# Gate and up projections by Strassen's seven block products in a hybrid attention kernel

## The chip, the core and the metric

The kernel runs on one core of one Trainium2 chip. The core has a tensor engine (PE, with its weight loads shown apart as PEld), a vector engine (DVE), a scalar engine (ACT), GpSimd (POOL), and a sync engine (SP) that issues the DMAs. Each engine works through its own queue in order and waits on semaphores for the others. The metric is the device time of one execution in microseconds. Before the change it is 2567.37 us, the median of three runs (2565.67 to 2568.33).

## The reference

Sixteen sequences of 512 tokens by 256 channels, all float32, go through four stages, each with a layer norm in front and a residual sum behind: a windowed attention (called a below), a feed-forward (f), a rotary attention (b), and the same feed-forward with the same weights again (h). The change is to the feed-forward:

```python
def _L0_ffn_ref(x, w_gate, w_up, w_down):
    DIM = 256
    HIDDEN = 768
    SCALE = 1.0 / 127.0
    wg = _dequant(w_gate, x.dtype)
    wu = _dequant(w_up, x.dtype)
    wd = _dequant(w_down, x.dtype)
    gate = jnp.einsum('bsd,hd->bsh', x, wg)
    up = jnp.einsum('bsd,hd->bsh', x, wu)
    h = jax.nn.silu(gate) * up
    return jnp.einsum('bsh,dh->bsd', h, wd)
...
x = x + _L0_attn_a_ref(_layernorm(x, axis=-1), ...)
x = x + _L0_ffn_ref(_layernorm(x, axis=-1), ...)
x = x + _L0_attn_b_ref(_layernorm(x, axis=-1), ...)
x = x + _L0_ffn_ref(_layernorm(x, axis=-1), ...)
```

## The kernel before, in words

**Order of the work.** The Python code does not emit its instructions in the order in which it is written. Every piece of work is a generator that yields an `Op` (an engine, a duration that the author assumes, what it needs, which buffers it takes and gives back). `Plan.run` keeps a clock per engine, always takes the operation that can start first on it (among those within a small window, by rank and then by `progress`, which the tables `LEAD`, `ENDS` and `SHARE` shift stage by stage), and only then lets the generator emit its instructions. So the queue order of every engine is fixed at build time by the planner's assumed durations, and on the chip each queue is followed strictly. All sixteen sequences are in flight as a pipeline over the four stages: while one sequence is in stage b, the next are in a and f and the one before is in h.

**PE fillers.** If the planner finds PE without work for over `FILL = 1.2` us, `Plan.run` calls `fill`, which emits `int((gap - 0.35) / 0.22)` matmuls of the identity with itself, 128 columns wide, whose result nobody reads.

**Ways in which PE is used.** A product of 128 by 128 weights with a moving operand can lie as one instruction on the whole array (FULL), or as four instructions on four strips of 32 output columns, which run side by side (COLS). Attention scores (`dn`, `nm`, `sa`) lie on four strips of 32 rows (ROWS). `product` (L485) emits the first two; an `Op` with `lying=FLEX` takes FULL or COLS, whichever suits what PE did last.

**PSUM.** It has eight banks of 512 float32 per partition. An operation that takes `"u"` gets one of them (six at most may be held so), one that takes `"s"` gets four, for the four strips of a score block. Dependences between the engines are tracked by tile, and a tile here is a whole bank.

**Feed-forward of one sequence** (`feed_forward`). `normalize` (L503) makes `xn` on DVE (L529), transposes it on PE into two banks (L563), and DVE (L571) and ACT (L573) copy one bank each into `xnt`, channels on the partitions, 512 tokens along the free dimension. Then for each of the six blocks of 128 hidden channels, `channels` emits two products of 512 columns (two blocks of input channels, summed in PSUM) for gate, and two for up. ACT takes tanh of half the gate (L1099), DVE multiplies (tanh + 1) by the gate (L1101), and DVE multiplies that by up into `ht` (L1107). When all six are done, four `project_out` calls, six products of 256 columns each, give the output, which DVE adds to the residual (L601). The last sequence's stage h goes in two halves of 256 tokens (`parts_of`), so that its end is shorter.

**Buffers.** Apart from constants, tiles live in slots that the planner hands out: `in_a`, `in_b`, `in_f` for `xnt` of the stages, `xn`, three `tmp`, four `pt` for transposed attention weights, two `ptb`, and so on.

Of the kernel before, what the change touches and what calls it, by code (L numbers as in the profile page):

```python
# [15 lines left out]
P = 128  # L16
S = 512
# [66 lines left out]
EARLY = {"us": 110.0}  # L84
BORDER = {"fr": 0.30, "fc": 0.15, "rf": 0.21, "rc": 0.13, "cf": 0.21, "cr": 0.21}
NEVER = 1e9

class Plan:
# [17 lines left out]
    def ready(self, op):  # L106
        at = 0.0
        for n in op.needs:
            at = max(at, self.at.get(n, NEVER) if isinstance(n, str) else n)
        for tag in op.takes:  # L110
            n = {"uu": 2, "s": 4}.get(tag, 1)
            if tag in ("u", "uu", "s"):
                at = max(at, sorted(self.slots["bank"])[n - 1])
            if tag != "s":
                at = max(at, sorted(self.slots["u" if tag == "uu" else tag])[n - 1])
        return at
# [7 lines left out]
    def take(self, op):  # L124

        for tag in op.takes:
            if tag == "s":
                op.k[tag] = [self.pick("bank") for _ in range(4)]
            elif tag in ("u", "uu"):
                op.k["u"] = [(self.pick("u"), self.pick("bank")) for _ in tag]  # L130
                op.k["u"] = op.k["u"] if tag == "uu" else op.k["u"][0]
            else:
# [9 lines left out]
    def progress(self, thread):  # L142

        _, _, stage, seq, _ = thread
        return seq + LEAD[stage] + ENDS.get(f"{stage}{seq}", 0.0) + self.done.get((stage, seq), 0.0) / SHARE[stage]

# [6 lines left out]
    def turn(self, op):  # L153
# [4 lines left out]
        return TURN[self.lying[0] + lying[0]]  # L158

    def run(self):  # L160
        while True:
# [17 lines left out]
            if first:  # L179
# [13 lines left out]
                <= least + (TURN["hold"] if engine == "pe" and self.lying == ROWS == c[1][1].lying else 0.05)  # L193
            ]
            if engine == "pe":
                start, t = min(
# [55 lines left out]
TURN = {"hold": 0.25, "fr": 0, "fc": 0.15, "rf": 0.2, "cf": 0.2, "rc": 0.05, "cr": 0.05}  # L252
LEAD = {"a": 0.0, "f": 0.741, "b": 1.33, "h": 2.645}

ENDS = {"b0": -0.05, "b2": -0.29, "h0": -0.04, "a0": 0.57, "a1": -0.08, "f15": -0.26, "h13": -0.11}
# [3 lines left out]
def kernel(  # L259
# [101 lines left out]
    def load_raw(ap, n, tag, name):  # L361
        raw = work.tile([P, n, ap.shape[1]], I32, tag=tag, name=f"raw_{name}")
        nc.sync.dma_start(raw, ap.rearrange("(c p) e -> p c e", p=P))
        return raw, const.tile([P, n, ap.shape[1]], F32, tag=name, name=name)

    raw_wg, wg_sb = load_raw(w_gate, NC, "ptb0", "wg_sb")
    raw_wu, wu_sb = load_raw(w_up, NC, "ptb1", "wu_sb")
    raw_wd, wd_sb = load_raw(w_down, NF, "ht0", "wd_sb")
# [49 lines left out]
    def dequantized():  # L418

        for at, t, raw, by, name in (  # L420
            (19.0, wg_sb, raw_wg, DEQUANT, "wg"),
            (22.0, wu_sb, raw_wu, DEQUANT, "wu"),
            (25.0, wd_sb, raw_wd, 0.5 * DEQUANT, "wd"),
        ):
            op = yield dve(0, at, us=0.9, makes=name, sbuf=True)
            if name == "wd":
                plan.slots["ht"] = [op.end]
            nc.vector.tensor_scalar(t, raw, by, None, ALU.mult)
# [4 lines left out]
    def values_bias():  # L433
# [3 lines left out]
        for kc in range(NC):  # L437
# [15 lines left out]
            "xn": 1,  # L453
            "in_a": 1,
            "in_b": 1,
            "in_f": 1,
            "tmp": 3,
            "pt": 4,
# [24 lines left out]
    input_of = {"a": "in_a", "b": "in_b", "f": "in_f", "h": "in_f"}  # L483
# [18 lines left out]

    def normalize(stage, b):  # L503
# [3 lines left out]
        slot = input_of[stage]  # L507
        for n, tokens in enumerate(parts_of(stage, b)):
# [3 lines left out]
            for t in tiles:  # L512
                op = yield dve(0, needs[t], us=0.51)
                if t == 0:
                    xt = xs[b]
                    stats = work.tile([P, NT, 6], F32, tag=f"stats_{stage}", name=f"stats_{me}")
                    mv = work.tile([P, NT, 2], F32, tag=f"mv_{stage}", name=f"mv_{me}")
                    rstd = work.tile([P, NT], F32, tag=f"rstd_{stage}", name=f"rstd_{me}")
                nc.vector.bn_stats(stats[:, t, :], xt[:, t, :])
                nc.vector.bn_aggr(mv[:, t, :], stats[:, t, :])  # L520
# [3 lines left out]
            takes = ("xn",) if n else ("xn", slot)  # L524
            op = yield dve(0, op.end, us=0.375 * len(tiles), takes=takes, sbuf=True)
            k_xn = op.k["xn"]
            xn = work.tile([P, NT, D], F32, tag="xn", name=f"xn_{me}_{n}")
            for t in tiles:
                nc.vector.tensor_scalar(  # L529
                    xn[:, t, :],  # L530
# [21 lines left out]
            else:  # L552
                plan.at[f"bias_{me}"] = 0.0
            for c in range(NC):
# [4 lines left out]
                    gives=(("xn", k_xn),) if c == NC - 1 else (),  # L559
                )  # L560
                ps = bank(op, [P, S], f"lt_{me}_{n}_{c}")
                for t in tiles:
                    nc.tensor.transpose(  # L563
                        ps[:, t * P : (t + 1) * P], xn[:, t, c * P : (c + 1) * P], ident
                    )
                if c == n == 0:
                    xnt[me] = work.tile([P, NC, S], F32, tag=slot, name=f"xnt_{me}")

                def keep(_, c=c, ps=ps, tokens=tokens):
# [5 lines left out]
                how = dict(gives=(("u", op.k["u"]),), makes=f"xnt_{me}.{n}.{c}")  # L575
                plan.start(
                    one((dve if c == 0 else act)(width, op.end, **how), keep), stage, b, -1
                )
# [3 lines left out]
        "f": ["wg", "wu", "wd"],  # L582
# [84 lines left out]
    def window_attention(b):  # L667
# [45 lines left out]
        yield from values("a", b, v_all, wv_sb, 0, v_lock, (("in_a", 0),))  # L713
# [181 lines left out]
    def weighted(b):  # L895
# [15 lines left out]
        def turns():  # L911
            for t in range(NT):
                for n, (oc, par) in enumerate(parts):
                    op = yield pe(0.44, f"sc_{me}.{t}.0", f"sc_{me}.{t}.1", takes=("u", "pt"))
# [9 lines left out]
                    def keep(_, t=t, n=n, on_dve=on_dve, ps=ps, op=op):  # L924
                        pt = buf(op, "pt", [P, 4, P], f"pt_{b}_{t}_{n}")
# [4 lines left out]
                        pts[t, n] = pt, op.k["pt"]  # L930
# [26 lines left out]
        for t in range(NT):  # L957
            go(weights(t))
            for ns in (range(4),):
# [10 lines left out]
                op.gives = [("pt", pts[t, n][1]) for n in ns]  # L970
# [45 lines left out]
    def global_queries(b, qg, keys, v_all, v_lock):  # L1016
# [30 lines left out]
        for c in range(NT):  # L1047
            nc.tensor.transpose(tp[:, c, :], gp[:, c * P : (c + 1) * P], ident[:R, :R])
        op = yield act(NT * R, op.end, takes=("pt",), gives=(("u", op.k["u"]),))
        pg = buf(op, "pt", [P, NT, R], f"pgq_{b}")  # L1050
# [8 lines left out]
            gives=(("pt", op.k["pt"]), (v_lock, 0)),  # L1059
# [27 lines left out]
    def feed_forward(stage, b):  # L1087
# [5 lines left out]
        def gated(f, n, tokens, gate, k, at):  # L1093

            width = tokens.stop - tokens.start
            op = yield act(width, at, takes=("tmp",))
# [472 lines left out]
```

## Time and profile before

| What | Value |
|---|---|
| median of the runs | 2567.37 us |
| the profiled execution, time | 2566.21 us |
| its span, first to last instruction | 2564.2 us |
| mean granted PE clock | 0.997 of full |
| PE busy | 99% of the span |
| DVE busy | 60% |
| ACT busy | 58% |
| POOL busy | 37% |
| gate and up products: 2916 records in stage f, 2388 in h | 184.6 + 184.4 and 183.7 + 184.2 us busy |
| DMA | 50.88 MB, mean 20 GB/s |

Busy time is the union of an engine's instructions. A float32 product shows as two records on PE for each instruction of the program (a transpose as one), and some of the records can be missing. Ends of matmuls are modelled, so the distance from one start to the next says more than the length of a record. Idle time is told apart by what ended it. A window names microseconds from the first instruction.

### The profile page before, as it was taken

The page shows a single profiled execution, that of the slowest core. Times are in us where ns is not written, and L with a number is a line of the kernel's source. Part 1 is how long each engine was busy: PE and PEld are TensorE (multiplying, and loading weights), DVE is VectorE, ACT ScalarE, POOL GpSimd, SP SyncE. Part 2 cuts the span into 40 slices and gives each one's busy share as a digit, 9 for nine tenths or more (in the row PEclk, how much of TensorE's full clock was granted, in tenths as well). Part 3 has the DMA queues.
Part 4 walks back from the last instruction along what each step waited for, and adds up shares of the span by engine and source line. Part 5 has one row for each costly group of instructions (what it writes and reads, how often), then busy time and mean ns, then how long its engine had stood idle before and what let it go on. Part 6 is the DMA issues. An engine that isn't in the chain of part 4 may idle for free.

```text
span 2564.2 us, 80282 instructions
## 1 busy us (share of the span) xinstructions
PE 2534.3 (99%) x35542; PEld 1276.8 (50%) x35542; DVE 1548.5 (60%) x3060; ACT 1481.6 (58%) x3697; POOL 949.6 (37%) x965
## 2 busy tenths in 40 slices
PE   8999999999999999999999999999999999999999
PEld 5655345454454544645445454454545446454436
DVE  7855658376573764937558474574846649466343
ACT  3656754736547475474745648466474754737473
POOL 5524245243450533524235251442604435242211
PEclk9999999999999999999999999999999999999999
DMA  4000010000100001010000100001000010100000
GB/s 142 25 25 2 2 41 2 18 25 2 42 2 25 19 2 41 2 37 7 16 28 2 41 2 25 19 2 41 2 25 19 2 41 2 33 2 2 10 9 10
DMA packets 26731, 50.88 MB, mean 20 GB/s; under 512 B 2384, under 2 KB 21264, under 8 KB 26384
## 3 DMA queue, kind: packets, MB, share of 16 engines
q1 hardware_dynamic: 25280, 45.23, 6.1%
q8 instruction: 278, 4.55, 0.7%
q10 hardware_dynamic: 1104, 0.53, 0.1%
q14 instruction: 69, 0.57, 0.1%
HBM read 13.77 MB, written 8.39 MB: 9 GB/s over the span
## 4 chain that ended last, share of the span: by engine, by line
PE 81%; DVE 14%; POOL 4%; issue 1%; ACT 0%; DVEq 0%; POOLq 0%; ACTq 0%
PE dn L1244 9%; PE po_h L489 7%; PE psc_gf L489 7%; PE psc_uf L489 7%; PE nm L1310 7%; PE psc_uh L489 6%; PE po_f L489 6%; PE yb L1378 5%; PE psc_gh L489 5%; DVE sm L839 2%; PE tp L920 2%; DVE sc L826 2%; PE psc_ka L489 2%; PE psv_a L489 2%; PE psc_qa L489 2%; PE po_b L489 2%
## 5 line engine op out<-in xcount | busy, mean ns | idle before, releaser
L1225 ACT ACTIVATE dn<-dn 128x512 f32<-128x512 f32 x1024 | 598.3, 584 | 137.1 <-PE dn L1244 135.8
L1276 ACT ACTIVATE ptb<-nm 128x512 f32<-128x512 f32 x640 | 329.2, 606 | 231.4 <-PE nm L1310 231.3
L1286 POOL TENSOR_SCALAR_AFFINE_SELECT ptb<-ptb 128x512 f32<-128x512 f32 x256 | 159.3, 637 | 565.0 <-ACT ptb L1276 553.1
L857 POOL TENSOR_TENSOR sc<-sc,sm 128x1056 f32<-128x1056 f32 x120 | 232.5, 1949 | 221.5 <-DVE sm L839 209.1
L1244 PE MATMUL dn<-kt,qb 32*128 32x512 f32 x2048 | 288.6, 634 | 0.3 <-DVE vb L632 0.2
L872 POOL TENSOR_TENSOR sc<-sc,sm 128x1056 f32<-128x1056 f32 x128 | 248.8, 1952 | 87.5 <-DVE sm L867 85.0
L864 ACT ACTIVATE sc<-sc 128x1056 f32<-128x1056 f32 x120 | 129.2, 1089 | 123.6 <-POOL sc L857 123.4
L1225 ACT ACTIVATION_READ_ACCUMULATOR dn<-dn 128x1 f32 x1024 | 191.6, 187 | 0.0
L489 PE MATMUL po_h<-wd_sb,ht_h 128*32 128x256 f32 (+1 forms) x2496 | 186.0, 380 | 0.6 <-issue 0.5
L489 PE MATMUL psc_uh<-xnt_h,wu_sb 128*32 128x512 f32 (+2 forms) x1188 | 184.2, 586 | 2.0 <-DVE th_h L1101 1.7
L489 PE MATMUL psc_gf<-xnt_f,wg_sb 128*32 128x512 f32 (+1 forms) x1464 | 184.6, 596 | 0.0
L489 PE MATMUL psc_uf<-xnt_f,wu_sb 128*32 128x512 f32 (+1 forms) x1452 | 184.4, 595 | 0.0
L489 PE MATMUL psc_gh<-xnt_h,wg_sb 128*32 128x512 f32 (+2 forms) x1200 | 183.7, 585 | 0.5 <-DVE xnt_h L571 0.3
L826 DVE TENSOR_TENSOR sc<-sa,mask 128x512 f32<-128x512 f32 x256 | 158.9, 680 | 41.2 <-PE sa L791 41.2
L1310 PE MATMUL nm<-qr,kr 32*128 32x512 f32 (+3 forms) x2048 | 181.9, 458 | 0.0
L489 PE MATMUL po_f<-wd_sb,ht_f 128*32 128x256 f32 (+1 forms) x2532 | 177.7, 380 | 0.6 <-issue 0.6
L1244 PEld LDWEIGHTS dn<-kt,qb 32*128 32x128 f32 x2048 | 87.4, 183 | 169.5 <-ACT dn L1225 53.3
L1378 PE MATMUL yb<-ptb,vb 128*32 128x256 f32 (+3 forms) x2080 | 165.7, 431 | 0.6 <-POOL ptb L1286 0.6
L866 DVE TENSOR_REDUCE sm<-sc 128x8 f32<-128x1056 f32 x120 | 148.8, 1240 | 26.8 <-ACT sc L864 26.8
L1101 DVE SCALAR_TENSOR_TENSOR th_f<-th_f,psc_gf 128x512 f32<-128x512 f32 x96 | 65.6, 683 | 162.4 <-ACT th_f L1099 162.3
L839 DVE TENSOR_REDUCE sm<-sc 128x8 f32<-128x1056 f32 x128 | 155.4, 1234 | 0.0
L1310 PEld LDWEIGHTS nm<-qr,kr 32*128 32x128 f32 x2048 | 92.3, 184 | 102.9 <-issue 59.7
(178 smaller groups left out, 4008.4 us busy)
## 6 DMA issues: line engine op xcount, KB each, us to landing
vw<-va SPq DMA_DIRECT2D x30, 576.0 KB, 5.5
out_dram<-x SPq DMA_DIRECT2D x16, 512.0 KB, 3.0
x<-in_x_dram SPq DMA_DIRECT2D x15, 512.0 KB, 4.0
vw<-va SPq DMA_DIRECT2D x30, 144.0 KB, 5.2
vw<-vb SPq DMA_DIRECT2D x2, 576.0 KB, 5.9
raw_wg_sb<-in_w_gate_dram SPq DMA_DIRECT2D x1, 768.0 KB, 10.2
raw_wu_sb<-in_w_up_dram SPq DMA_DIRECT2D x1, 768.0 KB, 9.4
raw_wd_sb<-in_w_down_dram SPq DMA_DIRECT2D x1, 768.0 KB, 11.0
```

Of the source, the lines that this page charges most:

```text
L489: nc.tensor.matmul(out[s], w[:, s], moving, skip_group_check=True, **how)
L826: nc.vector.tensor_tensor(flat[:, 4 * j : 4 * j + 4, 0:P], ps[j].rearrange("p c two w -> p (c two) w"), mask.unsqueeze(1).to_broadcast([P, ...
L839: nc.vector.tensor_reduce(small[:, 0, hs], part, AX.X, ALU.max, negate=True)
L857: nc.gpsimd.tensor_tensor(part, part, small[:, 0, hs].unsqueeze(2).to_broadcast([P, H // 2, P + NG]), ALU.add,)
L866: nc.vector.tensor_reduce(small[:, 1, hs], part, AX.X, ALU.add)
L872: nc.gpsimd.tensor_tensor(part, part, small[:, 1, hs].unsqueeze(2).to_broadcast([P, H // 2, P + NG]), ALU.mult,)
L1225: nc.scalar.activation(ps[j], ps[j], AF.Exp, scale=SCALE, accum_out=den[:, t, h : h + 1])
L1244: nc.tensor.matmul(ps[j], tiles["qb"][rows, par, oc, t * P : (t + 1) * P], tiles["kt"][rows, oc, :], start=True, stop=True,)
L1276: nc.scalar.activation(pt[:, j, :], ps[j], AF.Exp, scale=SCALE)
L1286: nc.gpsimd.affine_select(out=pt[:, :, at : at + P], in_=pt[:, :, at : at + P], pattern=[[0, 4], [1, P]], compare_op=ALU.is_ge, fill=0.0, ...
L1310: nc.tensor.matmul(ps[j][:, at : at + n], tiles["kr"][rows, oc, c * P : (c + 1) * P], tiles["qr"][rows, par, oc, c * P :], start=True, sto ...
L1378: nc.tensor.matmul(ps[rows, lo : part.stop], vb[:, c, 4 * oc + j, par : par + 2, :], pt[:, j, at + lo - c * P : at + part.stop - c * P], s ...
```

## The change

Gate and up of one block of 128 hidden channels are one product of two by two blocks: the weights in quarters (gate or up, first or second 128 input channels), the input in quarters (first or second 128 channels, first or second half of the tokens). Strassen's algorithm in Winograd's form makes it with seven block products in the place of eight, each 256 columns wide, with sums ahead of them and behind them.

- **Weights, once:** `wgu` holds seven combinations of the quarters (`dequantized`), made by six DVE instructions in the place of two; `wd_sb` stays.
- **Inputs, per sequence and stage:** `xnt` of f and h holds seven blocks of 256 columns (`combined`): ACT copies three, DVE makes four differences out of the two transposed banks.
- **Products, per block:** a first PE operation of four products into the halves of two banks (`g`, `u`), then the sums in `summed`: ACT copies the first into `th`, DVE makes `u2`, `s1`, writes two sums back into the banks, ACT writes a third one back, and a second PE operation adds the last three products to three of the four half banks. Then `gated` follows as before.
- **Buffers:** a block takes two banks at once (`"uu"`), one `tmp` from the start of the first PE operation to the end of `gated`, and one of three `pair` slots. `xn` and `pt` become `tmp`s (six in all; `xn` takes two at once), `in_a` and `in_b` become `in_ab`, `rden` is gone, `stats` is one small tile.
- **Planner:** other values in `TURN`, `LEAD`, `ENDS`, `EARLY`; `spared` and `NUDGE` are there but switched off (`keep` is 0, `NUDGE` empty).

```diff
-EARLY = {"us": 110.0}
+EARLY = {"us": 130}
...
-TURN = {"hold": 0.25, "fr": 0, "fc": 0.15, "rf": 0.2, "cf": 0.2, "rc": 0.05, "cr": 0.05}
-LEAD = {"a": 0.0, "f": 0.741, "b": 1.33, "h": 2.645}
-ENDS = {"b0": -0.05, "b2": -0.29, "h0": -0.04, "a0": 0.57, "a1": -0.08, "f15": -0.26, "h13": -0.11}
+TURN = {"hold": 0.35, "fr": 0, "fc": 0.3, "rf": 0.05, "cf": 0.02, "rc": 0, "cr": 0.1, "soon": 0.05, "keep": 0, "due": 0.0}
+LEAD = {"a": 0.0, "f": 0.907, "b": 1.74, "h": 2.504}
+ENDS = {"b0": 0.12, "b2": -0.05, "h0": -0.04, "a0": 0.57, "a1": 0.1, "f15": -0.26, "h13": -0.12, "b15": -0.29, "h14": 0.1, "h1": -0.07, "a12": 0.01, "b14": 0.08}
+RANK = {"sum": 0, "gate": -1, "pairs": 3}
...
+        g0, g1, u1, s1, s2, s3, s4 = (wgu[:, i, :] for i in range(7))
+        yield dve(0, 19.0, us=0.9, sbuf=True)
+        nc.vector.tensor_scalar(wgu[:, 0:2, :], raw_wg, DEQUANT, None, ALU.mult)
+        yield dve(0, 22.0, us=0.5, sbuf=True)
+        nc.vector.tensor_scalar(u1, raw_wu[:, 1, :], DEQUANT, None, ALU.mult)
...
+        nc.vector.scalar_tensor_tensor(s1, u0, DEQUANT, u1, ALU.mult, ALU.add)
...
+        nc.vector.scalar_tensor_tensor(s3, u0, -DEQUANT, g0, ALU.mult, ALU.add)
...
+        nc.vector.tensor_tensor(s2, s1, g0, ALU.subtract)
...
+        nc.vector.tensor_tensor(s4, g1, s2, ALU.subtract)
...
-            "xn": 1,
-            "in_a": 1,
-            "in_b": 1,
+            "in_ab": 1,
             "in_f": 1,
-            "tmp": 3,
-            "pt": 4,
+            "tmp": 6,
+            "pair": RANK["pairs"],
...
+    def combined(me, n, tokens, pss, at):
+        (ps0, k0), (ps1, k1) = pss
...
+        def copied():
+            op = yield act(w, f"lt_{me}.{n}", makes=f"x11_{me}.{n}")
+            nc.scalar.copy(to[:, 0, :], ps0[:, lo])
+            op = yield act(2 * w, at, makes=f"xnt_{me}.{n}.0")
+            nc.scalar.copy(to[:, 1:3, :], ps1[:, tokens].rearrange("p (two w) -> p two w", two=2))
+
+        def differences():
+            t1, t2, t3, t4 = (to[:, i, :] for i in (3, 4, 5, 6))
+            yield dve(w, f"lt_{me}.{n}", f"x11_{me}.{n}", sbuf=False)
+            nc.vector.tensor_tensor(t1, ps0[:, hi], to[:, 0, :], ALU.subtract)
+            yield dve(w, at)
+            nc.vector.tensor_tensor(t2, ps1[:, hi], t1, ALU.subtract)
+            op = yield dve(w, f"xnt_{me}.{n}.0", gives=(("u", k0),))
+            nc.vector.tensor_tensor(t3, to[:, 2, :], ps0[:, hi], ALU.subtract)
+            op = yield dve(w, gives=(("u", k1),), makes=f"xnt_{me}.{n}.1")
+            nc.vector.tensor_tensor(t4, ps1[:, lo], t2, ALU.subtract)
...
+        def third(w, dst, src, at, name):
+            yield act(w, at, makes=name)
+            nc.scalar.copy(dst, src)
...
+        def summed(f, n, tokens, gate, up, th, k, k_th, k_pair, at):
+            w = (tokens.stop - tokens.start) // 2
+            lo, hi = slice(tokens.start, tokens.start + w), slice(tokens.start + w, tokens.stop)
+            each = 0.43 * w / 256
+            op = yield act(w, at - 3 * each)
+            s1, u2 = th[:, lo], th[:, hi]
+            nc.scalar.copy(s1, gate[:, lo])
+            op = yield dve(w, op.end, at - 2 * each)
+            nc.vector.tensor_tensor(u2, gate[:, hi], s1, ALU.add)
+            op = yield dve(w, op.end - LAG["dve"], at - each)
+            nc.vector.tensor_tensor(s1, up[:, lo], u2, ALU.add)
+            there = f"u3_{me}.{f}.{n}"
+            go(third(w, up[:, lo], s1, op.end, there), RANK["sum"])
+            op = yield dve(w, op.end - LAG["dve"], at)
+            nc.vector.tensor_tensor(gate[:, hi], up[:, hi], u2, ALU.add)
+            ready = op.end
+            op = yield dve(w, op.end - LAG["dve"])
+            nc.vector.tensor_tensor(up[:, hi], up[:, hi], s1, ALU.add)
+            left[0] -= 1
+            gives = (("in_f", 0),) if not left[0] else ()
+            op = yield pe(3 * each, ready, there, gives=gives, lying=FLEX)
+            for out_, i, x_in in ((gate[:, lo], 1, 1), (gate[:, hi], 6, 2), (up[:, lo], 2, 6)):
+                product(out_, wgu[:, i, f * P : (f + 1) * P], inputs(n, w, x_in), op.lying, start=False, stop=True)
+            go(gated(f, n, tokens, gate, up, k, th[:, tokens], k_th, k_pair, op.end - each), RANK["gate"])
...
             for f in range(NF):
-                takes = ("u",) if f or n else ("u", "ht")
-                op = yield pe(us, *fed(me, n), takes=takes, lying=FLEX)
+                takes = ("uu", "tmp", "pair") if f or n else ("uu", "tmp", "pair", "ht")
+                op = yield pe(0.43 * 4 * w / 256, *fed(me, n), takes=takes, lying=FLEX)
...
-                gate = channels(op, xnt[me], wg_sb, f * P, f"g{me}_{f}_{n}", tokens)
-                go(gated(f, n, tokens, gate, op.k["u"], op.end))
...
-                up = channels(op, xnt[me], wu_sb, f * P, f"u{me}_{f}_{n}", tokens)
...
+                for out_, i, x_in, start in (
+                    (gate[:, lo], 0, 0, True),
+                    (gate[:, hi], 4, 4, False),
+                    (up[:, lo], 5, 5, True),
+                    (up[:, hi], 3, 3, False),
+                ):
+                    product(out_, wgu[:, i, f * P : (f + 1) * P], inputs(n, w, x_in), op.lying, start=start, stop=False)
+                th = buf(op, "tmp", [P, S], f"th_{me}_{f}_{n}")
+                go(summed(f, n, tokens, gate, up, th, op.k["u"], op.k["tmp"], op.k["pair"], op.end), RANK["sum"])
```

## The prediction, made before the changed kernel had run

> **What bounds the kernel now.** I read the page first: busy shares, the slices, then PE's own waits, then the timeline of a stretch in the middle.
>
> ```profile
> span 2564.2 us, 80282 instructions
> PE 2534.3 (99%) x35542; PEld 1276.8 (50%) x35542; DVE 1548.5 (60%) x3060; ACT 1481.6 (58%) x3697; POOL 949.6 (37%) x965
> ...
> PE   8999999999999999999999999999999999999999
> ...
> PEclk9999999999999999999999999999999999999999
> ```
>
> PE is busy in every slice, and the clock is granted throughout. The longest wait of PE on anything is 2.3 us (`psv_a`, on DVE, once, in the ramp). In the window 1067 to 1223 us, one period of the pipeline (in the chain of waits the `po_b` runs start at 1034.09, 1189.92 and 1345.70 us, 156 apart), PE is busy 155.90 of 156. So PE's queue sets the time: removed PE work counts in full, added PE work too, and DVE and ACT count only where PE stands and waits for them.
>
> What PE work costs is read from starts, not from lengths (the ends are modelled):
>
> ```profile
> 1001.30 1.92 PE L489 MATMUL psc_gf<-xnt_f,wg_sb 128*32 128x512 f32 x16
> ...
> 1003.15 1.14 PE L1310 MATMUL nm<-qr,kr 32*128 32x512 f32 x8
> ...
> 1004.23 1.92 PE L489 MATMUL psc_uf<-xnt_f,wu_sb 128*32 128x512 f32 x16
> ...
> 1005.97 1.90 PE L489 MATMUL psc_gf<-xnt_f,wg_sb 128*32 128x512 f32 x16
> ```
>
> Up to gate with nothing between is 1.74 us for two 512-wide products, which I round to the 1.72 of whole runs in the chain: 0.86 each. Where PE changes from column strips to row strips it takes 1.85 (0.13 more), and back again the four row strips take 1.08 where 0.86 is their work (0.22 more). A border costs 0.17 on average.
>
> **The products.** A 256-wide product is half a 512-wide one if nothing is fixed in it:
>
> ```profile
> 394.15 3.45 PE po_b L489 x64
> ```
>
> 64 records are eight 256-wide products in column strips: 0.431 each. So four products of 512 (3.44 us) become seven of 256 (3.01 us), 0.43 saved per block of 128 hidden channels. There are 16 sequences x 2 stages x 6 blocks = 192 such blocks (the last sequence's halves count as one): **-82.6 us**, all on PE.
>
> **What PE gets in return.** The order of the built programs shows two things that the diff doesn't. First, fillers: the program of before has 7 runs of them with 69 matmuls, the changed one 48 runs with 308. They run whether or not the gap that the planner saw is there on the chip.
>
> ```profile
> 2479.70 1.38 PE L1455 MATMUL fill<-ident 128*128 128x128 f32 x10
> ...
> 2524.18 2.72 PE L1455 MATMUL fill<-ident 128*128 128x128 f32 x22
> ```
>
> Ten records (five fillers) take 1.38 us, 22 take 2.72: 0.25 per filler. 239 more: **+60 us**. 114 of the 239 stand ahead of the third sequence's stage b (in the first attentions, and between score blocks `dn` that have no other work between them any more), 61 behind the start of stage b of sequence 14, and in the steady part 5 recur in every period. Some of those in the first 100 us replace waits that PE has today: all its waits there sum to 15 us, many ended by DVE, which is 96% busy from 50 to 100 us; I let that offset the six DVE weight sums at the start (about 3 us more DVE there), and book neither. Second, borders between the three ways of lying: 991 before, 1061 after, 70 x 0.17 = **+12 us**. PE's queue as a whole: -82.6 + 60 + 12 = -10.6 us. In the steady part (12 blocks, 5 fillers and 6 borders a period) it gains 5.16 - 1.25 - 1.0 = 2.9 us each time; the ramps give back most of that.
>
> **What PE will wait for.** DVE per block: four sums of 256 columns; the near row is the residual sum, also one PSUM operand and one in SBUF.
>
> ```profile
> L601 DVE TENSOR_TENSOR x<-x,po_b 128x256 f32<-128x256 f32 x64 | 24.6, 400 | 1.0 <-PE po_b L489 0.8
> L1005 ACT COPY yt<-ya 128x256 f32<-128x256 f32 x64 | 23.2, 362 | 37.1 <-PE ya L489 37.0
> ```
>
> 192 x 4 x 0.41 = 315 us, and four differences for one copy of 0.68 in each of 32 norms, 32 x 0.96 = 31: DVE goes from 1548 to about 1895 us, 74%. ACT adds two copies of 0.36 per block and some 0.4 per norm, about 150 us, to 64%. On average both hide beside PE. POOL and the DMAs get nothing to do. Sums written back to PSUM are in no row; ACT writing `dn` in place in PSUM (584 ns) against `nm` to SBUF (606) makes me take the same price, bounds 0.9 and 1.5 times.
>
> The chain from the first PE operation to the second decides. In the code ACT may copy the first product while PE makes the other three, and the last sum on DVE needs nothing from ACT. The built program's waits say otherwise: the copy waits for both products of its bank; ACT's write-back of the third sum waits for DVE's sum out of the same bank; and DVE's last sum, queued in order, waits for that write-back. The Trainium skill ("PSUM — Partial Sum Buffer", section "PSUM bank collisions raise a hardware error") says why: two engines may not be in one bank and quadrant at once, even at other columns, so waits have to be by bank. The trace of before has this too:
>
> ```profile
> DVE qa L663 <- ACT q L687: 35.1, 23, 4.0
> ```
>
> There DVE and ACT read the same bank, both only reading, and DVE stands for ACT, 1.5 us a time. By the code's view of halves no wait would arise and the sum ends at -10.6; by the rule I walk through a steady stretch. Hand-overs are from the timeline: PE to ACT or DVE 0.24, DVE to PE 0.06 (2527.43 + 0.42 to 2527.91), others 0.04; successive DVE rows of this size start 0.33 apart, dependent ones 0.45.
>
> In stage f the order is three first operations, then three second ones. From the first one's start they end at 1.72, 3.44, 5.16; the second ones should start at 5.16, 6.45 and 7.74. ACT's order has the write-back of block 0 behind its copy of block 2, which waits for that block's second product: 4.30 + 0.24 = 4.54, so the write-back runs 4.79 to 5.16 and DVE, standing at block 0's last sum, moves on at 5.20. Block 1's chain then takes 5.54 to 6.74, so the second operation starts at 6.80, 0.35 late; block 2's has its own write-back ahead of it and ends at 8.72: 8.78 in place of 8.09, 0.69 late, and 0.08 more for its last product. That is 1.1 us. In stage h of the same period the same walk finds one late start of 0.55 (block 3, DVE queue full with `xn`, `xnt_a` and rotary work), and none elsewhere. **1.7 us a period, 13 periods: +22 us.** The ramps have more such groups of three (f15, h13, h14, h15 at the end, f0 and f1 at the start, seven or eight): **+8 us**. I found no lack of banks: two for a block, three blocks at most, fit six.
>
> **Sum:** 2564.2 - 10.6 + 30 = 2583.6 us of span. The profiled execution took 2566.21, 2.0 more than its span and 1.2 under the median: **2586 us**, 0.7% slower. For changes of this kernel 0.2% (5 us) is about the least a measurement can tell.
>
> **The rivals.**
> - *The waits are hidden*: ACT and DVE get through the banks in time because the planner ordered PE around them, as before, when PE waited 24 us in all. Against it: the write-backs that I found in the built order. It gives 2566.2 - 10.6 = 2556, faster by 0.4%. With half of my waits it would be 2571, no difference to speak of. 0.21 for below 2562, 0.15 for within 0.2%.
> - *All the PE gain arrives* (fillers only fall where PE would stand anyway, now as before): 2566 - 83 = 2484. Against it: PE waits 24 us today; 60 us of filler can't all fall there. 0.02, in the 0.21.
> - *DVE becomes the bound.* In each block DVE stands about 0.45 us for ACT's write-back, 192 x 0.45 = 86 us on top of 1895, or 77% of the span, and near all in the feed-forward stretches, where its queue was already full in my walk. From the point at which DVE's queue there is longer than PE's, each group of three loses its 1.1 us and more: 64 groups x 1.1 = 70 where I booked 30, so 2626. 0.2.
> - The likeliest, 2573 to 2605: 0.44.
>
> So faster 0.21, same 0.15, slower 0.64. Low end 2548: the hidden-waits case with DVE-to-PSUM sums cheap. High end 2632: DVE-bound with sums at 1.5 times their price.
>
> **What would show it.** In the changed profile: `fill` with 616 records; the products of gate and up 578 us of starts (192 x 3.01) and their borders; PE busy still 98 to 99%, as fillers count; among PE's waits, second operations waiting for DVE's sum into gate, 0.3 to 0.7 us each, in total near 30 us; DVE waiting for ACT's write-back 0.4 to 2 us at a time, some 90 us or more. The period should be 154 to 155 us where it was 156. I am wrong if PE's waits stay near 24 us (then faster), or if the second operations wait over 60 us (then the third rival).

## The result, and the profile after

The changed kernel takes **2663.64 us** (median of four runs, 2659.52 to 2666.9), beside 2566.76 for the kernel before: a ratio of **1.0376, 95% interval 1.0358 to 1.0394**. It is 97 us slower, not the 20 that were forecast, and lies above the range of 2548 to 2632. The page of the changed kernel, with busy shares and the slices that answer to those shown of before:

```profile
span 2662.6 us, 87058 instructions
PE 2582.3 (97%) x38006; PEld 1537.5 (58%) x38006; DVE 1847.8 (69%) x3955; ACT 1616.9 (61%) x4126; POOL 942.2 (35%) x965
...
PE   9899999999999999999999999999999999999998
DVE  7974757669486784957769486785957769487334
...
PEclk9999999999999999999999999999999999999999
```

PE stands 80 us (span less busy) where it stood 30. The clock is granted as before (0.996). What PE waits for, in us, times and longest:

```profile
PE g_f L535 <- DVE g_f L1223: 17.5, 35, 2.9
PE g_h L535 <- DVE g_h L1223: 14.5, 22, 1.5
PE lt_h L624 <- DVE xn_h L588: 8.3, 13, 0.7
PE yb L1526 <- DVE sc L922: 5.4, 12, 0.5
```

The two top rows are the second PE operations waiting for DVE's sum into gate: 32.0 us, which the prediction had at "near 30". That looks like a hit and is not one, as will be seen. Pricing every PE instruction of the built order by the prediction's rows, from start to start, gives work of 2511.9 us before and 2501.1 after: -10.8, as predicted (-10.6). This sums the same prices anew, so it checks the counting; for the prices speaks the steady part of the kernel before, where they leave 3.6 us of 1558.5 unexplained (first row below). What the queue took beyond its work went from 46 to 155 us: **+109 where +30 were booked**. (The page shows only part of it as idle: ends are modelled, and a matmul that stands can count as busy.) The same split over the ten periods from the scores of sequence 3 to those of sequence 13:

```
                       time     work   fillers   beyond
before                1558.5   1554.9     0.0      3.6
after                 1598.0   1513.2    14.1     70.7
no sums, no copies    1554.8   1513.2    14.1     27.5
no write-back         1563.0   1513.2    14.1     35.8
DVE writes back       1592.4   1513.2    14.1     65.2
sums beside           1636.6   1513.2    14.1    109.4
before, half load     1582.7   1554.9     0.0     27.8
before, full load     1630.7   1554.9     0.0     75.9
```

Work fell by 41.7 us in ten periods, just what the prediction's 5.16 less 1.0 a period gives, and fillers rose by 1.4 a period where 1.25 were booked. The column "beyond" decides: 6.7 us more a period, not 1.7. The other rows belong to the experiments below.

### The profile page after: what moved, and what is told of

The parts are those of the page before. It is cut to its first block, busy times and chain, and to the rows that moved or that the text cites. A ratio compares the mean times of both kernels' runs of the same rounds, so it can differ in the third digit from the quotient of the medians.

```text
span 2662.6 us, 87058 instructions
## 1 busy us (share of the span) xinstructions
PE 2582.3 (97%) x38006; PEld 1537.5 (58%) x38006; DVE 1847.8 (69%) x3955; ACT 1616.9 (61%) x4126; POOL 942.2 (35%) x965
## 4 chain that ended last, share of the span: by engine, by line
PE 67%; DVE 26%; ACT 3%; issue 3%; POOL 1%; DMA 0%; DVEq 0%; ACTq 0%; SPq 0%; POOLq 0%
PE dn L1392 9%; PE po_h L535 7%; PE po_f L535 6%; PE nm L1459 5%; PE yb L1526 5%; PE g_h L535 4%; PE g_f L535 4%; PE u_h L535 3%; PE tp L1016 3%; DVE sc L922 2%; PE u_f L535 2%; PE fill L1603 2%; DVE sm L935 2%; PE psc_qa L535 2%; PE psv_a L535 2%
## 5 line engine op out<-in xcount | busy, mean ns | idle before, releaser
L1392 PE MATMUL dn<-kt,qb 32*128 32x512 f32 x2048 | 300.8, 637 | 1.0 <-DVE th_h L1201 0.2
L535 PE MATMUL g_f<-xnt_f,wgu 128*32 128x256 f32 (+1 forms) x2628 | 206.7, 383 | 21.7 <-DVE g_f L1223 17.5
L535 PE MATMUL g_h<-xnt_h,wgu 128*32 128x256 f32 (+2 forms) x1656 | 205.6, 376 | 14.8 <-DVE g_h L1223 14.5
L1459 PE MATMUL nm<-qr,kr 32*128 32x512 f32 (+3 forms) x2048 | 195.6, 461 | 0.7 <-issue 0.3
L535 PE MATMUL po_h<-wd_sb,ht_h 128*32 128x256 f32 (+1 forms) x2928 | 179.5, 383 | 0.5 <-DVE xnt_f L670 0.4
L535 PEld LDWEIGHTS g_h<-xnt_h,wgu 128*32 128x32 f32 (+1 forms) x1656 | 129.6, 136 | 69.1 <-issue 23.9
L535 PEld LDWEIGHTS g_f<-xnt_f,wgu 128*32 128x32 f32 (+1 forms) x2628 | 99.6, 114 | 114.7 <-DVE g_f L1223 32.6
L535 PE MATMUL u_f<-xnt_f,wgu 128*32 128x256 f32 (+1 forms) x1914 | 162.3, 382 | 0.0
L535 PE MATMUL u_h<-xnt_h,wgu 128*32 128x256 f32 (+2 forms) x1242 | 160.8, 374 | 0.7 <-DVE u_h L1226 0.7
L535 PEld LDWEIGHTS po_h<-wd_sb,ht_h 128*32 128x32 f32 (+1 forms) x2928 | 98.0, 112 | 95.1 <-ACT dn L1373 28.1
```

Of the source, the lines that this page charges most:

```text
L535: nc.tensor.matmul(out[s], w[:, s], moving, skip_group_check=True, **how)
L1392: nc.tensor.matmul(ps[j], tiles["qb"][rows, par, oc, t * P : (t + 1) * P], tiles["kt"][rows, oc, :], start=True, stop=True,)
L1459: nc.tensor.matmul(ps[j][:, at : at + n], tiles["kr"][rows, oc, c * P : (c + 1) * P], tiles["qr"][rows, par, oc, c * P :], start=True, sto ...
```

## The experiments

The theory formed on this trace: DVE, with the added sums and standing in its in-order queue for ACT's write-back, comes late in the feed-forward stretches, so that second operations start later than walked, and PE waits for other things queued behind as well. Rivals: the fillers cost what they were priced at; banks and shared buffers hold PE up; the planner's order doesn't fit the waits.

**Fillers out.** In the filler function only the first run is emitted:

```diff
         filled.append(n)
+        if len(filled) > 1:
+            return
```

> The changed kernel with every queue in the same order, but without its filler matmuls (the first run of 30 at the start stays; 278 of 308 go, priced at 0.25 us each, 70 us; 39 of the 69 of before stood there too). If the fillers fall where PE has other work waiting, as the prediction booked them, the time drops by about 60 to 70 us, to 2595-2605. If they fall mostly where PE would stand for a late DVE anyway, it drops by 10 to 25 us only, to 2640-2655, and PE's idle time grows by what the fillers held. If they keep something the kernel needs (the granted clock), the time rises.

Measured: 2668.69 us, ratio 1.040 (1.0385 to 1.0416): nothing gained. Two things go together here: the fillers stood in gaps, and the clock is lower without them. Windows of the changed kernel, then of this one (busy PE, PEld, DVE, ACT, POOL; PE's granted clock third from the end):

```profile
50.00:100.00 50.00, 42.93 (x1082) 34.73 (x1080) 46.84 (x87) 28.61 (x96) 31.59 (x28) 0.93 0.12 32
200.00:250.00 50.00, 49.13 (x755) 28.01 (x747) 16.82 (x42) 41.51 (x130) 2.05 (x4) 1.00 0.01 2
```

```profile
50.00:100.00 50.00, 37.17 (x998) 29.77 (x999) 45.20 (x86) 27.32 (x92) 32.19 (x28) 0.78 0.13 32
200.00:250.00 50.00, 49.48 (x691) 29.49 (x687) 17.36 (x44) 42.05 (x133) 2.55 (x4) 0.85 0.01 2
```

The granted clock falls from 0.93 to 0.78 and from 1.00 to 0.85; over the whole span from 0.996 to 0.986, 1% of 2660 or some 27 us if all of it is PE's time. The 278 fillers taken out, some 70 us of matmuls, stood in gaps of the plan. Without them the gaps stay, and PE's clock is lower in some stretches. How much of the 70 us each of the two takes back isn't told apart.

**Sums out.** ACT's first copy, the four DVE sums and ACT's write-back of each block are not emitted:

```diff
-            nc.scalar.copy(s1, gate[:, lo])
-            nc.vector.tensor_tensor(u2, gate[:, hi], s1, ALU.add)
-            nc.vector.tensor_tensor(s1, up[:, lo], u2, ALU.add)
-            nc.vector.tensor_tensor(gate[:, hi], up[:, hi], u2, ALU.add)
-            nc.vector.tensor_tensor(up[:, hi], up[:, hi], s1, ALU.add)
-            nc.scalar.copy(dst, src)
```

> The changed kernel with every queue in the same order, but the four DVE sums and the two ACT copies of every block left out, so that the seven products are made and never combined (fillers, borders, shared buffers, planner values all stay). Theory 1, the sums' load on DVE and ACT and the waits they bring are what is missing: the time falls to the sum of PE's queue with the waits of before, 2550-2572, and PE's idle time goes from about 80 us back to 25-35. Theory 2, two banks held per block from the first operation on, and shared buffers, hold PE up: it stays above 2630. Theory 3, half and half: about 2610.

Measured: 2584.03 us, ratio 1.0068 (1.0052 to 1.0085). The sums and what hangs on them cost 80 us of the 97. But the time lies above what the first theory gave: without the sums the kernel is still 18 us slower than before, where PE has 11 us less work and should be faster. In the new order PE waits elsewhere too. Its two longest waits here:

```profile
PE lt_h L624 <- DVE xn_h L588: 8.4, 13, 0.7
PE yb L1520 <- DVE sc L922: 5.4, 12, 0.5
```

They are those of the full kernel to a tenth: the new order puts them there, not the sums. (The shared buffers and the four differences of each norm are still in this kernel.)

This run is also the yardstick for the next three, which have the same PE instructions in the same order. The distance from each PE start to the next can be compared one by one, and the difference put down to the instruction that came late (us against the run without sums):

```
                     second operations   other PE work    all
no write-back              20.7               5.7         26.4
changed kernel             55.3              24.8         80.1
DVE writes back            69.1               6.1         75.2
sums beside                25.9             110.5        136.4
```

So the second operations cost 55 us, not the 32 that the view of waits shows, and 25 more are lost at other work, most of it outside gate and up.

**Write-back out.** Only `third`'s copy goes, so DVE's last sum stands for nobody.

```diff
         def third(w, dst, src, at, name):
             yield act(w, at, makes=name)
-            nc.scalar.copy(dst, src)
```

> The changed kernel with every queue in the same order, but ACT's write-back of the third sum into up is left out (that half of up lacks a term), so DVE's last sum no longer stands for ACT. If DVE's standing for the write-back (61 us in the changed kernel's trace) is what makes DVE late, the time falls by 40 us or more, to 2600-2625. If the number of sums does it, it falls by less than 20, to 2645-2660.

Measured: 2608.09 us, ratio 1.0165 (1.015 to 1.0181): 55.6 us less, for 61.0 us of standing removed, the two rows of DVE's waits in the changed kernel:

```profile
DVE u_f L1226 <- ACT u_f L1193: 36.9, 59, 1.1
DVE u_h L1226 <- ACT u_h L1193: 24.1, 51, 1.1
```

DVE still makes the same sums (busy 1841.0 us). PE's waits in this kernel show where the gain came from:

```profile
PE lt_h L624 <- DVE xn_h L588: 8.2, 13, 0.8
PE yb L1525 <- DVE sc L922: 5.4, 12, 0.5
PE g_h L535 <- DVE g_h L1222: 4.8, 11, 1.5
PE g_f L535 <- DVE g_f L1222: 4.0, 4, 2.6
```

By the table, the second operations lose 34.6 us less and other work 19.1 less: an engine that stands in its queue is late for both. The sums that are left cost 26. ACT has 55 us less to do here too, but so it has in the next run, where the time does not fall.

**DVE writes back itself.** Is it the round trip through ACT, or only that DVE is held up?

```diff
             nc.vector.tensor_tensor(s1, up[:, lo], u2, ALU.add)
+            nc.vector.tensor_tensor(up[:, lo], up[:, lo], u2, ALU.add)
...
-            nc.scalar.copy(dst, src)
```

> The changed kernel with every queue in the same order, but the third sum is written back into up by DVE itself, as a fifth sum right behind its own third one, and ACT's write-back is gone; everything is computed. DVE no longer stands for ACT (61 us in the changed kernel) but carries 198 sums more of 0.42 us (83 us). If it is the standing, and the round trip DVE to ACT to PE, that makes PE late, the time falls towards the kernel without the write-back (2608): 2610 to 2635. If it is only how long DVE is held up in all, by work or by standing, it rises by the difference: 2665 to 2690.

Measured: 2659.41 us, ratio 1.0362 (1.0346 to 1.0377), not to be told from the changed kernel, and neither of what was expected. The table shows two effects that cancel. Other work is nearly free of waits (6.1 us for 24.8), as DVE no longer stands. But DVE's extra sum lies ahead of its sum into gate, for which the second operation waits: 198 chains are 0.42 us longer, and the second operations lose 69 us for 55.

**Sums beside the banks.** The same number of sums and copies, but on `th` alone; only ACT's first copy touches a bank.

```diff
-            nc.vector.tensor_tensor(u2, gate[:, hi], s1, ALU.add)
+            nc.vector.tensor_tensor(u2, s1, s1, ALU.add)
...
-            nc.vector.tensor_tensor(gate[:, hi], up[:, hi], u2, ALU.add)
+            nc.vector.tensor_tensor(u2, u2, u2, ALU.add)
```

> The changed kernel with every queue in the same order and as many sums and copies of the same width, but they read and write only the scratch tile in SBUF, never the two banks, except ACT's first copy out of gate (the products are not combined). So DVE and ACT carry nearly the same load, and DVE no longer stands for ACT's write-back because of a bank, nor PE's second operation for DVE's sum into the bank. If the load alone makes DVE late, the time stays near 2640-2664. If the hand-overs through the bank are the loss, it falls close to the kernel without sums, 2555-2590.

Measured: 2722.71 us, ratio 1.0611 (1.0596 to 1.0627), beyond both. Two things were not as expected. The standing didn't go (60.8 us of it), as source and target of ACT's copy are now in DVE's tile. And the sums got slower: the costliest one, in h and in f (413 and 415 ns in the changed kernel):

```profile
L1217 DVE TENSOR_TENSOR th_h<-th_h 128x256 f32<-128x256 f32 x90 | 54.4, 605 | 4.9 <-ACT th_h L1215 4.8
...
L1217 DVE TENSOR_TENSOR th_f<-th_f 128x256 f32<-128x256 f32 x96 | 44.3, 461 | 78.1 <-ACT th_f L1215 78.0
```

So DVE is busy 1913.0 us, 65 more. The miss tells something all the same: no second operation waits for a sum here (their longest wait, 14.6 us, is for ACT's first copy), and still the kernel is slower, because 110 us are lost at other work, most of it behind a DVE that is late in its queue. As the sums also got slower, this run is no clean test of the load. Its longest PE waits:

```profile
PE g_h L535 <- ACT th_h L1215: 14.6, 12, 1.6
PE pgp L1046 <- DVE th_h L1201: 8.9, 11, 0.8
PE lt_h L624 <- DVE xn_h L588: 8.0, 13, 0.7
PE g_h L535 <- DVE xnt_a L633: 7.8, 11, 0.7
PE tp L1016 <- DVE th_h L1201: 7.7, 2, 5.1
```

**The load in the kernel before.** Products, buffers, and order stay; each block gets four DVE sums that nobody reads, then in another run two:

```diff
             nc.vector.tensor_tensor(ht[:, f, tokens], th, up[:, tokens], ALU.mult)
+            w = width // 2
+            scr = work.tile([P, S // 2], F32, tag="scr", name=f"scr_{me}_{f}_{n}")
+            for _ in range(4):
+                nc.vector.tensor_tensor(scr[:, :w], up[:, tokens.start : tokens.start + w], th[:, :w], ALU.add)
```

> The kernel before with every queue in the same order, and four sums of 256 columns more on DVE behind each block's product of gate and up, read from up's bank, written to a scratch tile that nobody reads: the change's DVE load (198 x 4 x 0.42 = 330 us) without its second PE operation, its copies or its buffers. If DVE's load by itself makes PE late, 2610 or more, and PE waits for DVE all over. If only the hand-overs inside a block do it, 2566 to 2580.

> The kernel before with every queue in the same order and two unread DVE sums of 256 columns behind each block, in place of four (four gave 2678). If the cost is in proportion to the load from the start, half of 111: 2615 to 2630. If it sets in only where DVE's queue gets longer than PE's, well under half: 2575 to 2600.

Measured: four sums 2677.97 us, ratio 1.0435 (1.0419 to 1.045); two sums 2599.48, ratio 1.0131 (1.0114 to 1.0148). Without one Strassen product, the added DVE work costs 111 us here, the first half 34, the second 77: more than in proportion. The page of the kernel with four, and its longest PE waits:

```profile
PE 2591.6 (97%) x35542; PEld 1294.4 (48%) x35542; DVE 1840.2 (69%) x3852; ACT 1485.3 (56%) x3697; POOL 948.5 (35%) x965
```

```profile
PE dn L1248 <- DVE scr_h L1111: 14.1, 21, 0.7
PE pgp L950 <- POOL pq L944: 14.0, 9, 1.6
PE psc_gh L489 <- DVE scr_h L1111: 9.3, 11, 1.2
PE po_f L489 <- DVE ht_f L1107: 4.5, 3, 2.4
```

DVE is at 69%, PE at 97%, as in the changed kernel, and scores, transposes and output products wait. One thing is mixed in: the unread sums read up's bank, so they also keep it from PE for longer, and the rows that name `scr` are waits for such a bank. All waits for `scr` come to 29 of PE's 76 us of waits in this view; all of PE's waits before came to 24. So added DVE work can do it with plain products, in an order made for less of it; load and bank are not told apart. The order of the changed kernel, made for more, takes a DVE of 1841 us (no write-back) with 26 us of loss.

**Order and buffers.** Eight runs asked what the planner and the buffers have to do with it. First ACT's write-back was started behind DVE's last sum:

```diff
-            go(third(w, up[:, lo], s1, op.end, there), RANK["sum"])
...
             nc.vector.tensor_tensor(up[:, hi], up[:, hi], s1, ALU.add)
+            go(third(w, up[:, lo], s1, op.end, there), RANK["sum"])
```

> The changed kernel with ACT's write-back started behind DVE's last sum in place of between its second and third sum, so that ACT waits for DVE at that bank and DVE never for ACT; everything is computed, and the planner orders anew around it. If DVE's standing for ACT (61 us) is what makes PE late, the time falls by 30 us or more, to 2600-2635. If the load of the sums is the cause, it stays within 15 us of 2664; the second PE operation then has a longer chain, 0.4 us more, which can make it slower still, up to 2690.

Measured: 2708.43 us, ratio 1.0556 (1.0541 to 1.0572). That is above all that was expected. DVE no longer stands for the write-back (its waits have no such row), but the planner made another order, with 464 fillers in place of 308, so this run doesn't test the wait. Nor does the next one, in which the planner was told of the built waits (2718.0, ratio 1.0589, 1.0573 to 1.0605):

```diff
-            op = yield act(w, at - 3 * each)
+            op = yield act(w, at - 2 * each)
...
+            go(third(w, up[:, lo], s1, op.end, there), RANK["sum"])
-            op = yield dve(w, op.end - LAG["dve"])
+            op = yield dve(w, there)
```

> The changed kernel with the same instructions, but the planner is told of the waits that the built program has (ACT's first copy waits for both products of its bank, its write-back for DVE's sum out of that bank, DVE's last sum for the write-back, the second PE operation for that sum), so it can lay other PE work between; values unchanged. If the planner's not knowing is the cause of the loss, 2600 to 2640. If the work simply has no better order with these banks and buffers, or the values fit only the order that they were made for, 2680 to 2720, as with the write-back moved behind the last sum.

How far such numbers are a matter of values that fit was measured with plain products: shared buffers with the old and the new values, and the kernel before with the new values (in each only the tables `TURN`, `LEAD`, `ENDS`, `EARLY` are exchanged).

> The changed kernel's shared buffers (one in_ab for the inputs of a and b, six tmp slots that also serve xn and pt) with the kernel before's eight plain products and its planner values. If sharing buffers costs nothing, 2560-2575 as before. If it is a good part of the 97 us, 2590 or more.

> As the one with plain products and shared buffers, but with the changed kernel's planner values (TURN, LEAD, ENDS, EARLY), which were not chosen for this work. Together with the other it tells how much of the time hangs on these values: if they matter little, within 10 us of the other; if they shift the order of the ramps and the steady part, 20 to 60 us above it.

> The kernel before, unchanged but for the changed kernel's planner values (TURN, LEAD, ENDS, EARLY). With the two runs of plain products in shared buffers (2694 with the old values, 2653 with the new) and the kernel before (2566) it completes a square. If the shared buffers alone cost, 2566 to 2590. If order is so finely set that other values cost as much by themselves, 2620 to 2670.

Measured: 2694.05 (ratio 1.0493, 1.0476 to 1.0511), 2652.9 (1.0338, 1.0323 to 1.0354) and 2607.14 (1.0155, 1.0138 to 1.0172). The kernel before loses 40 us by other values alone. So a run with unfitted values says nothing of buffers, and values were searched for three kernels, with the planner's own clock as the measure:

> Eight plain products in the changed kernel's shared buffers, as in the run that took 2694, but with planner values found for it by a search over some 1600 orders on the planner's own clock. If the shared buffers cost time whatever the order, 2640 or more. If the 128 us were only values that didn't fit, 2565 to 2590.

> The changed kernel whose planner knows the waits of the built program, as in the run that took 2718, with values found for it by the same search. If the order was the loss, and an order that knows the waits can hide them, 2560 to 2600. If the DVE work of the sums has to be paid in any order, 2620 to 2660.

> The seven products with no sums, DVE and ACT work of these and their waits left out of the program and of the plan (the products are not combined), two banks per block and shared buffers kept, values found by the same search. If banks and buffers are what hold PE up, it stays near the run without sums in the changed kernel's order, 2560 to 2590. If they cost little, the saving of the products arrives: 2505 to 2535.

Plain products in shared buffers came to 2584.62 us (1.0072, 1.0057 to 1.0087): shared buffers cost at most 19 us, the old run's other 109 were values. The planner that knows the waits, with fitted values, came to **2616.23** (1.0198, 1.0183 to 1.0214), between what was expected if an order can hide the waits and if it can't: such an order recovers 47 of the 97 us, with the same DVE work (1844.1 busy) and 23 us of standing for the write-back where it was 61; how much of that is the knowing and how much the values isn't told apart. Its longest PE waits:

```profile
PE g_h L535 <- DVE g_h L1222: 10.7, 11, 1.0
PE u_h L535 <- DVE u_h L1226: 6.7, 19, 0.7
PE ya L535 <- DVE pg L1050: 2.1, 1, 2.1
```

`lt_h` and `yb` are no longer among these; but it is still 50 us slower than before. The products without sums in an order of their own missed (2631.31, 1.0256, 1.024 to 1.0271): the chip didn't follow the planner's clock, PE waits for `xn_b` (16.4 us) and `xnt_b` (15.5), and the granted clock is 0.985. What banks and buffers alone would leave of the saving stays open.

## Why the prediction was wrong

- **The work of PE's queue was right.** Undisturbed blocks of the trace take 0.86 + 0.86 and 0.86 + 0.43 us for the first and second operation, the 3.01 that was booked; 616 filler records; -10.8 us for -10.6.
- **Fillers** were booked at their full 60 us. As part of the queue's length that holds; as a cost that could be saved it doesn't: their removal gained nothing, at a lower clock.
- **The term that failed** is that of PE's waits, 30 us booked for 109. It falls into four parts, from the differences of starts between the changed kernel, the run without sums, and the kernel before:
  - *"1.7 us a period, 13 periods: +22 us"* came to 36.5. The mechanism was right and its sizes short: blocks 1 and 2 of the group in f are late by 0.45 and 0.79 us in the mean of ten periods (0.35 and 0.69 walked), stage h's block 3 by 0.88 (0.55); and *"none elsewhere"* was wrong: 0.14 at block 5 of f and 0.12 at block 2 of h. (Block 4 of f has a mean of 0.26, but from single pauses, one of 1.8 us that ended by no wait in the trace; in most periods it is on time.)
  - *The ramps, "+8 us"*, came to 18.7.
  - *Nothing was booked for other work behind DVE*; the sums cost 24.8 there. In one period `og` is late by 0.42, `yb` by 0.62, `po_f` by 0.23, all on time without the sums.
  - *Before's 46 us beyond the work were assumed to stay.* Without any sums there are 75: 29 more come with the new order, its shared buffers and its differences, such as the 8 us of `lt_h`. Which of the three has what share stays open.
- **The premise behind the third part** was "On average both hide beside PE". An average was the wrong view. Windows of 12 us of the kernel before (third figure: DVE), at the end of the period that the prediction had read:

```profile
1187.00:1199.00 12.00, 12.00 (x191) 8.11 (x184) 11.62 (x29) 3.34 (x4) 8.12 (x6) 1.00 0.01 3
1199.00:1211.00 12.00, 12.00 (x258) 9.46 (x257) 11.86 (x30) 2.89 (x7) 6.62 (x7) 1.00 0.01 3
1211.00:1223.00 12.00, 12.00 (x40) 6.55 (x38) 11.93 (x21) 6.59 (x10) 8.93 (x6) 1.00 0.00 0
```

DVE was already full for 36 us of this period, without holding PE up. In the changed kernel:

```profile
1093.00:1105.00 12.00, 12.00 (x70) 6.97 (x72) 11.68 (x28) 4.62 (x11) 6.11 (x6) 1.00 0.01 1
1105.00:1117.00 12.00, 11.36 (x169) 7.57 (x161) 11.83 (x23) 10.44 (x28) 10.27 (x8) 1.00 0.01 2
1117.00:1129.00 12.00, 12.00 (x98) 9.47 (x89) 10.83 (x28) 5.01 (x13) 5.31 (x5) 1.00 0.01 3
1129.00:1141.00 12.00, 11.29 (x144) 7.97 (x147) 11.17 (x26) 6.08 (x16) 0.00 (x0) 1.00 0.01 1
```

Full, or nearly so once its standing is counted, for 48 us on end, and PE stands beside it. The stretch reaches into stage h: here the added load falls where DVE had the least room, and a figure per stretch would have said so. But in stage f of the same period, where second operations lose even more (the 0.45, 0.79 and 0.14 above, beside 0.88 and 0.12 in h), DVE is not full:

```profile
1177.00:1189.00 12.00, 11.18 (x200) 5.83 (x192) 7.34 (x18) 6.46 (x18) 0.00 (x0) 1.00 0.28 90
```

It waits there, 3.4 us for ACT's first copy and 1.6 us for the write-back. Without the write-back, `g_f` waits 4.0 us where it waited 17.5: most of this loss is the chain of dependent steps that the prediction walked, and no share of busy time shows it.

- **The third rival**, DVE as the bound of the feed-forward stretches, was nearest, at 0.2, and too small at 2626: it charged only groups of three, 64 times 1.1 us. Its 70 us is the right size for the sums (80.1), but the 29 of the order were missing there too. The sign set for it, second operations waiting over 60 us, would have misled: the view of waits shows 32 where the starts show 55.
- The other terms: DVE 1847.8 us where about 1895 were forecast, ACT +135 for +150, DVE's standing 61 for 90. All smaller than booked; the time came from where they fell. (The last sum of the prediction, 2583.6 + 2.0 + 1.2, is 2586.8; 2586 was written.)
- The waits by bank, for which the rule of the Trainium skill ("PSUM — Partial Sum Buffer", section "PSUM bank collisions raise a hardware error") was weighed against the code's view by halves, are in the trace, and removing the largest of them (the write-back) gave 55.6 us. Taking the rule rather than the halves was right; no run here shows what the chip does without the waits.

## What to carry to other kernels

Work added to an engine that isn't the bound is to be priced per stretch: take the windows in which it already is full, add the work and the standing that fall there, and charge the bounding engine for everything that this in-order queue serves, not for the new consumers alone. Walk the chains of dependent steps besides: in stage f they made PE wait while DVE had room. Where two runs have the same queue order, compare starts one by one; a view of waits can show little more than half of what a late operand costs. And in a kernel whose order is planned, a new order brings waits of its own: values alone moved this kernel by 40 us, so fit them again before an algorithm or a buffer is blamed.

## What the runs showed of the hardware

- **DVE in SBUF beside POOL.** The groups of the layer norm's 256-column operation, in h and in f of the changed kernel:

```profile
L588 DVE TENSOR_SCALAR xn_h<-x,mv_h,rstd_h 128x256 f32<-128x256 f32 x64 | 37.2, 644 | 0.2 <-POOL rstd_h L576 0.2
...
L588 DVE TENSOR_SCALAR xn_f<-x,mv_f,rstd_f 128x256 f32<-128x256 f32 x64 | 24.5, 442 | 0.0
```

Of the 64 in h, 54 run with POOL busy for over half of their time and take 689 ns in the mean, the other ten 404 ns; in the kernel before 12 of 64 met POOL. The sums that were moved to SBUF in stage h are another case: of the 90 full-width ones at L1217, 14 met POOL and took 1633 ns on average, the other 76 took 415. In the changed kernel, where all four sums read a bank, the 92 of stage h that met POOL took 418 ns, the others 422. This agrees with the Trainium skill ("SBUF — State Buffer", section "Who interferes with whom"), by which DVE in its two-port modes, or with two inputs in SBUF while GpSimd reads there, and GpSimd take one pair of ports in turn; in which mode `xn` ran, the trace doesn't say. `lt_h` waits for `xn_h` 8.3 us in the changed kernel; that this meeting with POOL is its cause was not tried by itself.
- **Without the fillers the granted clock falls.** Windows of the run without fillers, in a stretch that read 1.00 with them:

```profile
230.00:240.00 10.00, 10.00 (x44) 6.71 (x37) 0.67 (x3) 10.00 (x35) 1.27 (x2) 0.73 0.00 1
240.00:250.00 10.00, 10.00 (x93) 6.78 (x92) 1.23 (x4) 9.22 (x26) 1.28 (x2) 0.50 0.01 2
```

PE is shown as busy throughout, but it starts only 44 matmuls in the first window, beside an ACT that is busy all the time. That the gaps between such starts are what lowers the clock fits both runs; it was not tried in another way.
